# Attention block on one core: the last group and the last feed-forward tiles in an order written by hand, the residual in W_base's diagonal, weight preparation at another unit

## The chip, the cores and the metric

The kernel runs on one core of a Trainium2 chip. The metric is the time of one execution on the device in microseconds (us). Three plain executions took 703.10, 703.36 and 704.18 us, median 703.36. A further execution was taken by the hardware profiler; all durations of single instructions are from that one.

## What is computed

Two batches (b) of 512 tokens with 512 features go through causal attention with 32 query heads and 8 key/value heads of 128, then a residual and a layer norm, then a feed-forward part of one base matrix and eight low-rank experts that a sparsemax router weighs, then a residual and a layer norm again. Cut to what matters:

```python
x = hidden                                      # (2, 512, 512), f32
q, k, v = x @ Wq, x @ Wk, x @ Wv                # 32 / 8 / 8 heads of 128
p = softmax(causal(q @ k.T * 128**-0.5))
x = layernorm(x + (p @ v) @ Wo)
base = x @ W_base.T + b_base
w = sparsemax(x @ W_router.T + b_router)        # 8 experts
h = einsum('bsd,edr->bser', x, lora_A)          # rank 16
x = layernorm(x + base + einsum('bser,bse,ero->bso', h, w, lora_B))
```

## The kernel before

**Precision.** Products of the attention are split into a high and a low f16 half, and each is made of three matmuls (`mm3`, L223): high-high, high-low, low-high. After every product, `cut_psum` (L227, L228) splits the PSUM result again: ScalarE (ACT) writes the high half, VectorE (DVE) the low one. The feed-forward part uses f32r halves in the same way.

**Units.** A *group* (g, b) is one key/value head g with its four query heads on one batch, a *unit* (g, b, i) the 128 query rows of tile i in it, so there are 64 units. The groups run as (0,0), (0,1), (1,0) ... (5,1), and then (6,0), (7,0), (6,1), (7,1); in the last group i goes from 3 down to 0, so that the largest tile comes first. Three functions make a unit:
- `unit_a` (L309): for four heads, the scores `s` (3 matmuls each, into 4 PSUM buffers "S"), mask and maximum on VectorE (L325), exp on ACT (L330); after every second head the reciprocal of the sums (L336, L338), the cut into `phl`, and a DMA transpose into `pt` on SyncE's queue (SP).
- `unit_b` (L353): `pv` from `pt` and `vt`, then its cut `o`.
- `unit_c` (L373): `pw` from `o` and Wo's rows, and `acc += pw * factor` on VectorE (L384). `acc` starts as x, so the residual is in it.

In step s the loop (L668) issues `unit_a` of unit s, a part of the next group's projections (`proj`, k, q, v), `unit_b` of unit s-1 and `unit_c` of unit s-2. A scheduler of the language decides the order on each engine from there, except in the first group's start, which stands in a block with a written order (L536).

**Weights.** `prepare` (L152) loads a group's six projection matrices (JS) or four Wo rows (ROWS) in raw form, takes the largest absolute value of each (`amax`, L118, VectorE), squares these on ACT (L180), adds over partitions with a matmul with ones (`tot`, L123, PE), makes scales of them (L128 to L133) and has GpSimd (POOL) scale and split the weights (L112 to L115). `plan` and `at` (L629 to L659) tell at which unit each step of such a generator is issued. `sync_load` ties a load behind the third-last transpose. `behind(engine)` (L407) ties what is issued in it behind the last instruction of that engine so far.

**Feed-forward.** After a tile's last `unit_c`, `ffn` (L422) is stepped once per place in the loop: layer norm statistics (L413 to L415, the power on POOL, L417), normalise (L420), `px`: four transposes, three copies (L431 to L433), POOL adds the bias to `acc` (L434), `pb`: LoRA and router product (L437), the router's sparsemax in ten small VectorE instructions (L453 to L463), `phw` and `h` (L469 to L472), `pa`: the base product and the LoRA product in one PSUM tile, `acc += pa` on VectorE (L477), layer norm to `y`, store on SP (L480). Tiles 0 to 3 are of batch 0 and run beside batch 1's attention; tiles 4 to 7 follow the last group, in the order 7, 6, 5, 4. In the profile's names `lna` and `lnb` are the first and second layer norm.

Of the kernel before, what the change touches and what calls it, by code (L numbers as in the profile page):

```python
# [8 lines left out]
F32 = mybir.dt.float32  # L9
# [27 lines left out]
def kernel(  # L37
# [131 lines left out]
    def measure(g, js, raws, name, rows, n):  # L169
        mx = sb.tile([P, 8], F32, tag="mx", name=f"mx{name}", bufs=2)  # L170
        for k, (j, raw) in enumerate(zip(js, raws)):
            j = k + 1 if rows else j
            amax(mx[:, j : j + 1], raw)
            if k % 2:
                yield
        sc = sb.tile([P, 2, 8], F32, tag="sc", name=f"sc{name}", bufs=8)
        if rows:
            amax(mx[:, 0:1], mx[:, 1:5])
        sq = sb.tile([P, 8], F32, tag="sq", name=f"sq{name}", bufs=2)
        nc.scalar.activation(sq[:, :n], mx[:, :n], AF.Square)  # L180
        scales(sc, total(sq, n, name), n)
        SC[(g, rows)] = sc
        yield
# [122 lines left out]

    PT = {}

    def unit_a(g, b, i):  # L309
        n = P * (i + 1)  # L310
        k2, lm = KT[(g, b)], LM[(g, b)]
        phl = sb.tile([P, 2, 2, 2, n], F16, tag="PHL", name=f"phl{g}_{b}_{i}", bufs=2)
        pt = sb.tile([P, 2, 2, 2, i + 1, P], F16, tag="PT", name=f"pt{g}_{b}_{i}", bufs=2)
        es = []
        st = sb.tile([P, 4, HPG], F32, tag="ast", name=f"ast{g}_{b}_{i}", bufs=3)
        for h in range(HPG):
            q2 = QT[(g, b, h)]
            sc = ps.tile([P, S], F32, tag="S", name=f"s{g}_{b}_{i}_{h}", bufs=4)
            qs = slice(i * P, (i + 1) * P)
            mm3(sc[:, :n], [  # L320
                (q2[:, 0, qs], k2[:, 0, :n]),
                (q2[:, 0, qs], k2[:, 1, :n]),
                (q2[:, 1, qs], k2[:, 0, :n]),
            ])
            nc.vector.tensor_tensor_reduce(  # L325
                out=sc[:, :n], in0=sc[:, :n], in1=mask[:, S - n :], scale=lm[:, h : h + 1], scalar=BIG,
                op0=ALU.add, op1=ALU.min, accum_out=st[:, 0, h : h + 1],
            )

            nc.scalar.activation(  # L330
                sc[:, :n], sc[:, :n], AF.Exp, bias=st[:, 0, h : h + 1], scale=-1.0, accum_out=st[:, 1, h : h + 1]
            )
            es.append(sc)
            if h % 2 == 0:
                continue
            nc.vector.reciprocal(st[:, 2, h - 1 : h + 1], st[:, 1, h - 1 : h + 1])  # L336

            nc.vector.scalar_tensor_tensor(  # L338
                st[:, 3, h - 1 : h + 1], st[:, 2, h - 1 : h + 1], 32768.0, sc[:, :2], ALU.mult, ALU.max
            )  # L340
            pair = h // 2
            for j in range(2):
                k = 2 * pair + j
                cut_psum(phl[:, pair, 0, j, :], phl[:, pair, 1, j, :], es[k][:, :n], st[:, 3, k : k + 1])

            sync_transpose(
                pt[:, pair].rearrange("p a h t q -> p (a h t) q"), phl[:, pair].rearrange("p a h n -> p (a h n)")
            )
        PT[(g, b, i)] = pt

    OT = {}

    def unit_b(g, b, i):  # L353
# [4 lines left out]
        for kt in range(i + 1):  # L358
            vh, vl = vt[:, kt, :], vt[:, NT + kt, :]
            ph, pl = pt[:, :, 0, :, kt, :], pt[:, :, 1, :, kt, :]  # L360
            pairs += [(vh, ph), (vh, pl), (vl, ph)]
        mm3(pv, pairs)
        o2 = sb.tile([P, 2, HPG, P], F16, tag="O", name=f"o{g}_{b}_{i}", bufs=2)
        cut_psum(o2[:, 0], o2[:, 1], pv, 2.0**-15)
        OT[(g, b, i)] = o2

    def out_factor(g, b):
        lm = LM[(g, b)]
# [4 lines left out]
    def unit_c(g, b, i, first):  # L373
# [5 lines left out]
        for h in range(HPG):  # L379
            w2 = W[(g, 6 + h)]  # L380
            pairs += [(o2[:, 0, h, :], w2[:, 0, :]), (o2[:, 0, h, :], w2[:, 1, :]), (o2[:, 1, h, :], w2[:, 0, :])]
        mm3(pw, pairs)
        a = acc[b * NT + i]
        nc.vector.scalar_tensor_tensor(a, pw, LM[(g, b)][:, 7:8], a, ALU.mult, ALU.add)  # L384

    F = {}

    def ffn_setup():
        base = [sb.tile([P, KC, HID], F32R, tag=f"base{q}", name=f"base{q}") for q in range(2)]
        for c in range(KC):  # L390
            split(base[0][:, c, :], base[1][:, c, :], load_raw(w_base[:, c, :], f"base{c}"))
            yield
        lar = sb.tile([P, KC, NL], F32, tag="lar", name="lar")
        sync_load(lar, lar_in)
# [13 lines left out]

        return tc.issue_after(next(i for i in reversed(nc.cur_bb.bb.instructions) if i.engine == engine))

    def layernorm(dst, src, name, tail):
        st = sb.tile([P, 12], F32, tag="lnst", name=f"ln{name}", bufs=2)
        nc.vector.bn_stats(st[:, 0:6], src)  # L413
        nc.vector.bn_aggr(st[:, 6:8], st[:, 0:6])
        nc.vector.tensor_scalar(st[:, 9:10], st[:, 7:8], EPS, None, ALU.add)  # L415
        with tc.high_priority():
            nc.gpsimd.tensor_tensor(st[:, 8:9], st[:, 9:10], cmh, ALU.pow)  # L417
        yield
        with nullcontext() if tail else behind(mybir.EngineType.DVE):
            nc.vector.tensor_scalar(dst, src, st[:, 6:7], st[:, 8:9], ALU.subtract, ALU.mult)  # L420

    def ffn(t, tail):  # L422
        base, lar, lb, bias, kk = F["base"], F["lar"], F["lb"], F["bias"], F["k"]
        a = acc[t]
        yield from layernorm(a, a, f"a{t}", tail)
        px = ps.tile([P, KC, P], F32, tag="S" if tail else "wo", name=f"px{t}", bufs=4 if tail else 1)
        for c in range(KC):
            nc.tensor.transpose(px[:, c, :], a[:, c * P : (c + 1) * P], ident)
        xf = sb.tile([P, KC, P], F32, tag="xf", name=f"xf{t}")
        x2 = sb.tile([P, 2, KC, P], F32R, tag="x2", name=f"x2{t}")  # L430
        nc.scalar.copy(xf, px)  # L431
        nc.scalar.copy(x2[:, 0], px)
        nc.vector.tensor_tensor(x2[:, 1], px, f(x2[:, 0]), ALU.subtract)  # L433
        nc.gpsimd.tensor_tensor(a, a, bias[:, :HID], ALU.add)  # L434
        yield
        pb = ps.tile([P, NL], F32, tag="S" if tail else "pj", name=f"pb{t}", bufs=4 if tail else 2)
        mm3(pb, [(xf[:, c, :], lar[:, c, :]) for c in range(KC)])  # L437

        def base_part():
            pa = ps.tile([P, HID], F32, tag="pj", name=f"pa{t}", bufs=2)  # L440
            pairs = []
            for c in range(KC):
                xh, xl = x2[:, 0, c, :], x2[:, 1, c, :]
                pairs += [(xh, base[0][:, c, :]), (xh, base[1][:, c, :]), (xl, base[0][:, c, :])]
            mm3(pa, pairs, last=False)
            return pa

        if tail:
            pa = base_part()
        r = sb.tile([P, 6, NE], F32, tag="rt", name=f"rt{t}", bufs=2)  # L450
        s = sb.tile([P, 4], F32, tag="rs", name=f"rs{t}", bufs=2)
        z, zs, zc, sup, tmp, w = (r[:, j, :] for j in range(6))
        nc.vector.tensor_tensor(z, pb[:, NE * NR :], bias[:, HID:], ALU.add)  # L453
        nc.vector.max(zs, z)
        nc.vector.tensor_tensor_scan(zc, zs, zs, 0.0, ALU.add, ALU.bypass)
        nc.vector.tensor_tensor(tmp, zs, kk, ALU.mult)
# [7 lines left out]
            hw, pb[:, : NE * NR].rearrange("p (e r) -> p e r", e=NE),  # L464
            w.unsqueeze(2).broadcast_to([P, NE, NR]), ALU.mult,
        )
        yield
        ph = ps.tile([P, P], F32, tag="S" if tail else "wo", name=f"phw{t}", bufs=4 if tail else 1)
        nc.tensor.transpose(ph, hw.rearrange("p e r -> p (e r)"), ident)  # L469
        h2 = sb.tile([P, 2, P], F32R, tag="h2", name=f"h2{t}")  # L470
        nc.scalar.copy(h2[:, 0, :], ph)
        nc.vector.tensor_tensor(h2[:, 1, :], ph, f(h2[:, 0, :]), ALU.subtract)  # L472
        yield
        if not tail:
            pa = base_part()
        mm3(pa, [(h2[:, 0, :], lb[:, 0, :]), (h2[:, 0, :], lb[:, 1, :]), (h2[:, 1, :], lb[:, 0, :])], first=False)
        nc.vector.tensor_tensor(a, a, pa, ALU.add)  # L477
        y = sb.tile([P, HID], F32, tag="y", name=f"y{t}", bufs=2)
        yield from layernorm(y, a, f"b{t}", tail)
        nc.sync.dma_start(out_rows[t], y)  # L480
        yield

    live = []

# [138 lines left out]

    def step_live():

        step_ffn(s < len(units) - NT + LC)


    plan = {u: [] for u in range(-1, len(units) + 3)}  # L629
# [23 lines left out]
    for g in range(1, NG):  # L653
        u = NT * (starts[g] - 2) - (3 if g == NG - 2 else 0)
        if g > 1:
            at(prepare(g, JS), u - 1, u, u, u + 1, u + 2, u + 2, u + 3, u + 3, u + 3)
        u += NT
        if g > 1:
            at(prepare(g, ROWS), u - 1, u, u + 1, u + 2, u + 2, u + 3, u + 3)  # L659
# [1 line left out]
    def advance(last=False):  # L661
        while plan.get(s):
            next(plan[s].pop(0), None)
            if not last:
                break

    LB, LC = 1, 2
    for s in range(len(units) + LC):  # L668
        if s < len(units):
            g, b, i = units[s]  # L670
            k = s // NT
            nx = groups[k + 1] if k + 1 < len(groups) else None
            if s == NT:
                load_x(1)
            unit_a(g, b, i)
            step_live()
            if nx:
                for j in ((4, 0), (1,), (5,), (2, 3))[i]:
                    proj(*nx, j)
                    advance()  # L680
            step_live()
        if s >= LB and s - LB < len(units):
            unit_b(*units[s - LB])
            step_live()
            advance()
        if s >= LC:
            n = s - LC
            u = units[n]
            unit_c(*u, n % NT == 0)
            step_live()  # L690
            if u == (NG - 1, 1, NT - 1):
                while live:
                    step_ffn(True)
            if u[0] == NG - 1:
                live.append(ffn(u[1] * NT + u[2], u[1] == NB - 1))
        advance(True)
    while live:
        step_ffn()


_OUTS = [((2, 512, 512), "float32")]
# [51 lines left out]
```

## Time and profile before

| what | value |
|---|---|
| plain executions | 703.10, 703.36, 704.18 us, median 703.36 |
| the profiled execution | 707.78 us |
| its span, first to last instruction | 705.7 us, 10,943 instructions |
| chain that ended last, by engine | PE 78%, DVE 8%, DMA 5%, issue 3%, ACT 3%, POOL 2% |
| its costliest lines | pw 20%, pq 18%, pv 13%, s 11%, pk 5%, pvp 5%, pa 2% |
| granted TensorE clock, mean | 0.995 of full |
| DMA issues on SP | 128 transposes of p (3.8 us from issue to landing), loads of 256 KB (3.0 to 5.2 us), 8 stores (2.0 us) |

Engines in the profile: PE is TensorE's matmul, PEld its weight load, DVE VectorE, ACT ScalarE, POOL GpSimd, SP SyncE. A row of a timeline is: start, duration, engine, line, operation, output <- inputs, shapes, count of merged instructions, and in brackets how long the engine was idle before and what ended that. A row of the view of waits is: the waiting engine, its tile and line, what it waited for, then the sum in us, the count, and the longest.

### The profile page before, as it was taken

Reading aid. Unit: us, or ns where it says so; the run is one execution under the profiler, and the core shown is the slowest. Engines: PE = TensorE matmul, PEld = TensorE weight load, DVE = VectorE, ACT = ScalarE, POOL = GpSimd, SP = SyncE. Lnnn points to the kernel's source line nnn. Section 1 sums busy time; section 2 is a strip of 40 time slices with the busy share of each in tenths; the row PEclk is TensorE's granted clock in tenths of the full one; section 3 lists DMA queues with packets and bytes.
Section 4 is the critical chain, followed back from the end, with each engine's and each line's share of the span. In section 5 each row is a group of like instructions: output and inputs, shape, how many; then the busy total and the mean of one; then the engine's idle time right before and its main releaser. Section 6 shows DMA issues by size and latency. Waiting matters only on the chain.

```text
span 705.7 us, 10943 instructions
## 1 busy us (share of the span) xinstructions
PE 681.4 (97%) x3434; PEld 351.9 (50%) x3434; DVE 534.4 (76%) x1604; ACT 366.4 (52%) x1010; POOL 241.3 (34%) x331
## 2 busy tenths in 40 slices
PE   8999999999999999999999999899999999998895
PEld 4764545454544545454444545354544554554463
DVE  5797787867777786867777868767785786878775
ACT  5875745555464555545554556345464563445410
POOL 7665450725026240825034193134322010100131
PEclk9999999999999999999999999999999999999999
DMA  8659382637456373856368362916443251435301
GB/s 322 178 117 193 78 201 47 140 76 173 75 109 142 65 183 42 174 111 150 75 129 185 62 148 48 199 24 149 75 91 74 56 106 32 93 62 117 61 16 45
DMA packets 202026, 78.08 MB, mean 111 GB/s; under 512 B 186736, under 2 KB 186736, under 8 KB 201968
## 3 DMA queue, kind: packets, MB, share of 16 engines
q1 hardware_dynamic: 201680, 76.85, 49.7%
q10 hardware_dynamic: 288, 0.52, 0.3%
q8 instruction: 27, 0.44, 0.3%
q14 instruction: 31, 0.25, 0.1%
HBM read 29.12 MB, written 2.10 MB: 44 GB/s over the span
## 4 chain that ended last, share of the span: by engine, by line
PE 78%; DVE 8%; DMA 5%; issue 3%; ACT 3%; POOL 2%; SPq 0%; POOLq 0%; DVEq 0%; ACTq 0%
PE pw L223 20%; PE pq L223 18%; PE pv L223 13%; PE s L223 11%; PE pk L223 5%; PE pvp L223 5%; PE pa L223 2%; DVE phl L228 2%; PE park L223 2%; DMA raw<-in_wv_dram 1%; DMA pt<-phl 1%; ACT s L330 1%; PE pb L223 1%; DVE acc L384 1%; DVE s L325 1%
## 5 line engine op out<-in xcount | busy, mean ns | idle before, releaser
L330 ACT ACTIVATE s<-s,ast 128x128 f32<-128x128 f32 (+3 forms) x256 | 127.7, 499 | 170.0 <-DVE ast L325 168.2
L223 PE MATMUL pw<-w,o 128*128 128x512 f16 x768 | 176.9, 379 | 1.3 <-DVE acc L384 1.3
L223 PE MATMUL pq<-xT,w 128*128 128x512 f16 x672 | 153.9, 382 | 2.6 <-DVE q L228 2.6
L223 PEld LDWEIGHTS <-w 128*128 128x128 f16 x1008 | 98.3, 98 | 115.2 <-issue 5.9
L227 ACT ACTIVATE phl<-s,ast 128x128 f16<-128x128 f32 (+3 forms) x256 | 116.8, 539 | 37.7 <-issue 20.0
L228 DVE SCALAR_TENSOR_TENSOR phl<-s,ast,phl 128x128 f16<-128x128 f32 (+3 forms) x256 | 125.0, 545 | 3.9 <-ACT phl L227 2.2
L325 DVE CUSTOM_DVE_ANT_0 s<-s,mask,lm 128x128 f32<-128x128 f32 (+3 forms) x256 | 126.7, 555 | 1.3 <-PE s L223 1.2
L223 PE MATMUL s<-k,q 128*128 128x128 f16 (+3 forms) x768 | 117.9, 299 | 4.7 <-DVE phl L228 3.9
L223 PEld LDWEIGHTS <-o 128*128 128x128 f16 x768 | 74.8, 98 | 91.2 <-issue 2.4
L223 PE MATMUL pv<-pt,vt 128*128 128x512 f16 x480 | 114.5, 379 | 2.7 <-DMA pt<-phl 2.7
L223 PEld LDWEIGHTS <-q 128*128 128x128 f16 x768 | 68.4, 98 | 53.1 <-issue 7.2
L255 POOL TENSOR_SCALAR lm<-sc,xs 128x1 f32<-128x1 f32 x15 | 4.0, 264 | 235.8 <-DVE sc L132 144.3
L115 POOL TENSOR_TENSOR w<-raw,w 128x512 f16<-128x512 f32 x68 | 77.2, 1154 | 0.3
L223 PEld LDWEIGHTS <-vt 128*128 128x128 f16 x480 | 46.8, 100 | 56.6 <-DMA pt<-phl 3.4
L384 DVE SCALAR_TENSOR_TENSOR acc<-pw,lm,acc 128x512 f32<-128x512 f32 x64 | 47.9, 749 | 31.8 <-PE pw L223 31.7
L228 DVE SCALAR_TENSOR_TENSOR o<-pv,o 128x512 f16<-128x512 f32 x64 | 43.9, 686 | 31.1 <-ACT o L227 31.0
L112 POOL TENSOR_SCALAR raw<-raw,sc 128x512 f32<-128x512 f32 x68 | 46.3, 691 | 59.7 <-DVE sc L133 59.6
L118 DVE TENSOR_REDUCE mx<-raw 128x1 f32<-128x512 f32 x66 | 44.3, 681 | 29.4 <-DMA raw<-in_wo_dram 13.3
L227 ACT ACTIVATE o<-pv 128x512 f16<-128x512 f32 x64 | 39.5, 617 | 32.3 <-PE pv L223 32.3
L330 ACT ACTIVATION_READ_ACCUMULATOR s<-s,ast 128x1 f32 x256 | 51.5, 201 | 0.0
L228 DVE SCALAR_TENSOR_TENSOR q<-pq,q 128x512 f16<-128x512 f32 x56 | 38.4, 687 | 14.6 <-ACT q L227 14.5
L227 ACT ACTIVATE q<-pq 128x512 f16<-128x512 f32 x56 | 34.0, 611 | 18.7 <-PE pq L223 18.7
(125 smaller groups left out, 613.0 us busy)
## 6 DMA issues: line engine op xcount, KB each, us to landing
raw<-in_wo_dram SPq DMA_DIRECT2D x32, 256.0 KB, 3.6
raw<-in_wq_dram SPq DMA_DIRECT2D x28, 256.0 KB, 4.6
raw_x<-in_xt_dram SPq DMA_DIRECT2D x8, 256.0 KB, 4.7
acc<-in_x_dram SPq DMA_DIRECT2D x8, 256.0 KB, 4.6
pt<-phl SPq DMA_TRANSPOSE x128, 3.8
out_dram<-y SPq DMA_DIRECT2D x8, 256.0 KB, 2.0
raw<-in_wk_dram SPq DMA_DIRECT2D x7, 256.0 KB, 3.0
raw<-in_wv_dram SPq DMA_DIRECT2D x7, 256.0 KB, 4.6
```

The costliest lines, as they stand in the source:

```text
L112: nc.gpsimd.tensor_scalar(view, view, by, 1.0, ALU.mult, ALU.mult)
L115: return first.ins, nc.gpsimd.tensor_tensor(lo, view, hi, ALU.subtract).ins
L118: nc.vector.tensor_reduce(dst, view, AX.X, ALU.max, apply_absolute_value=True)
L223: nc.tensor.matmul(dst, a, b, start=first and j == 0, stop=last and j == n - 1)
L227: nc.scalar.activation(hi, psrc, AF.Copy, scale=by)
L228: return nc.vector.scalar_tensor_tensor(lo, psrc, by, hi, ALU.mult, ALU.subtract).ins
L255: engine.tensor_scalar(lm[:, 4:5], sc[:, 0, 4:5], XS[b][0], 1.0, ALU.mult, ALU.mult)
L325: nc.vector.tensor_tensor_reduce(out=sc[:, :n], in0=sc[:, :n], in1=mask[:, S - n :], scale=lm[:, h : h + 1], scalar=BIG, op0=ALU.add, op1= ...
L330: nc.scalar.activation(sc[:, :n], sc[:, :n], AF.Exp, bias=st[:, 0, h : h + 1], scale=-1.0, accum_out=st[:, 1, h : h + 1])
L384: nc.vector.scalar_tensor_tensor(a, pw, LM[(g, b)][:, 7:8], a, ALU.mult, ALU.add)
```

## The change

1. **The tail.** The loop ends four units earlier (`len(units) - NT`). The last group's units, the last parts of the group before it, the feed-forward of tile 3 and of tiles 4 to 7 are cut into pieces and issued in the order of a list of tokens, `TAIL`, in a block in which each engine keeps the written order. `unit_a`, `unit_b` and `unit_c` become generators for that; the ordinary loop runs them through with `done`.
2. **The residual** goes into the base matrix: the identity is added to W_base's diagonal before it is split, so `pa` holds the residual too. For tiles 0 to 2 one VectorE addition of `pa` and the bias replaces L434 and L477. For tiles 3 to 7 the bias enters PSUM as two matmuls of a one-partition row (`bias_row`), and statistics and normalise read `pa` in PSUM. The base product's order becomes xh with base0, xh with base1, xl with base0, four matmuls each, and the low half of x is made on VectorE (`low`, tile 7) or on POOL (`low_pool`, tiles 3, 4, 5 and 6).
3. **Weights.** The JS generator's first step is put at unit u-2, where it was at u-1 (for group 6 it stays), and JS's maxima of groups 2 to 7 are issued behind VectorE's last instruction.

```diff
@@ measure
-            amax(mx[:, j : j + 1], raw)
+            with behind(mybir.EngineType.DVE) if g > 1 and not rows else nullcontext():
+                amax(mx[:, j : j + 1], raw)
...
@@ ffn_setup
-            split(base[0][:, c, :], base[1][:, c, :], load_raw(w_base[:, c, :], f"base{c}"))
+            raw = load_raw(w_base[:, c, :], f"base{c}")
+            diag = raw[:, c * P : (c + 1) * P]
+            nc.gpsimd.tensor_tensor(diag, diag, ident, ALU.add)
+            split(base[0][:, c, :], base[1][:, c, :], raw)
...
+    def low_pool(t):
+        px, xf, xh, xl = X[t]
+        nc.gpsimd.tensor_tensor(xl, xf, f(xh), ALU.subtract)
...
+    def base_part(t, last):
...
+        pairs = list(F["row"]) if last else []
+        for x2, r in ((xh, 0), (xh, 1), (xl, 0)):
+            pairs += [(x2[:, c, :], base[r][:, c, :]) for c in range(KC)]
+        mm3(PA[t], pairs, last=False)
...
+    def store(t, src, st):
+        y = sb.tile([P, HID], F32, tag="y", name=f"y{t}", bufs=2)
+        normalize(y, src, st)
+        nc.sync.dma_start(out_rows[t], y)
...
-            at(prepare(g, JS), u - 1, u, u, u + 1, u + 2, u + 2, u + 3, u + 3, u + 3)
+            at(prepare(g, JS), u - (1 if g == NG - 2 else 2), u, u, u + 1, u + 2, u + 2, u + 3, u + 3, u + 3)
...
+    def bias_row():
...
+        split(rows[0][0:1, :], rows[1][0:1, :], bias)
+        nc.gpsimd.tensor_scalar(rows[2][0:1, :P], ones[0:1, :], 1.0, 1.0, ALU.mult, ALU.mult)
+        F["row"] = [(rows[2][0:1, :P], rows[q][0:1, :]) for q in (0, 1)]
...
+    TAIL = """
+    n3 a7 N3 p7 q7 B7 C6 O7 x3 D6 a6 r3 C7 L3 s3 p6 q6 b7 o7 a5 D7 m3 p5 q5 h3 c7 a4 b6 d7 p4 o6
+    n7 e3 N7 q4 c6 x7 d6 b5 n6 f3 r7 l7 o5 m7 N6 s7 c5 d5 h7 x6 b4 e7 n5 o4 f7 N5 r6 L6 c4 F7 d4
+    F3 x5 s6 n4 m6 h6 L5 r5 N4 s5 e6 f6 m5 h5 F6 x4 e5 L4 r4 s4 f5 m4 h4 F5 e4 f4 F4
+    """
...
-    for s in range(len(units) + LC):
+    for s in range(len(units) - NT):
...
-    while live:
-        step_ffn()
+        if s == len(units) - 2 * NT:
+            bias_row()
+    while live:
+        step_ffn(True)
+    with tc.manual_schedule(engines={ET.PE, ET.DVE, ET.Activation, ET.Pool, ET.SP}):
+        tail()
```

The tokens, with the tile's number behind: a scores with mask, maximum and exp; p and q the cut and transpose of the first and second pair of heads; b and o `pv` and its cut; c and d `pw` and its addition to `acc`; B, O, C, D the same for the group before the last; n and N first statistics and normalise; x the transposes and copies; l and L the low half of x on VectorE or POOL; r `pb`; s the router; m the base product; h `phw` and `h`; e the LoRA product; f and F second statistics, and normalise with store.

## Prediction

> **What bounds the kernel now.** I read the page first: busy times, then the row of slices.
>
> ```profile
> PE 681.4 (97%) x3434; PEld 351.9 (50%) x3434; DVE 534.4 (76%) x1604; ACT 366.4 (52%) x1010; POOL 241.3 (34%) x331
> PE   8999999999999999999999999899999999998895
> ```
>
> TensorE (PE) is the bound: 24 us of 705.7 are idle. So the question for every edit is which PE wait it ends. The last three slices are the weak ones. I then took PE's busy time by stretch (columns: length, PE, PEld, DVE, ACT, POOL busy with counts, clock, DMA):
>
> ```profile
> 400.00:450.00 50.00, 50.00 (x254) 24.20 (x253) 38.71 (x113) 27.93 (x78) 24.35 (x32) 1.00 0.56 123
> 450.00:500.00 50.00, 47.42 (x241) 22.82 (x240) 38.17 (x108) 23.86 (x66) 23.81 (x32) 0.97 0.52 105
> ...
> 635.00:650.00 15.00, 12.66 (x63) 7.21 (x61) 13.14 (x45) 10.34 (x26) 1.27 (x1) 1.00 0.52 106
> 650.00:665.00 15.00, 13.18 (x76) 6.79 (x75) 11.57 (x42) 6.82 (x26) 0.98 (x2) 1.00 0.49 88
> 665.00:680.00 15.00, 13.11 (x64) 7.58 (x64) 10.94 (x33) 3.91 (x9) 3.96 (x5) 1.00 0.13 35
> 680.00:690.00 10.00, 9.62 (x55) 7.54 (x54) 7.35 (x35) 1.83 (x4) 3.61 (x4) 1.00 0.01 4
> 690.00:698.00 8.00, 7.22 (x35) 5.22 (x33) 5.21 (x22) 1.12 (x3) 0.55 (x1) 1.00 0.09 33
> ```
>
> Most stretches of the body are full; 450 to 500 is not, and its clock fell. From 635 to 698 PE is busy 55.8 of 63 us, so 7.2 us are idle. Each wait also hides the drain of the matmul before it (a 512-column f16 matmul lasts 0.38 us but the next starts 0.216 us after it). Counted from start to start in the timeline, the waits from 635 on sum to 10.1 us: 1.4 + 0.5 before the scores of tile 6, 1.4 around px3 and pb3, 0.3 before pw of tile 6, 1.8 for the transposes of tile 5, 0.8 before pb7, 1.3 before pw of tile 4, 1.9 around the last four LoRA steps, and 0.6 in three small ones.
>
> The waits in the body come from the view of who waited for whom, and then from the timeline around the largest:
>
> ```profile
> DVE mx L118 <- DMA raw<-in_wk_dram: 12.0, 6, 3.0
> DVE mx L118 <- DMA raw<-in_wq_dram: 4.0, 6, 1.3
> ...
> PE pq L223 <- DVE q L228: 2.6, 1, 2.6
> ```
>
> ```profile
> 450.44 0.69 DVE L118 TENSOR_REDUCE mx<-raw 128x1 f32<-128x512 f32 x1 [0.86 <-DMA raw<-in_wq_dram]
> 451.04 1.40 DVE L228 SCALAR_TENSOR_TENSOR phl<-s,ast,phl 128x512 f16<-128x512 f32 x2
> 452.36 0.15 DVE L338 SCALAR_TENSOR_TENSOR ast<-ast,s 128x2 f32<-128x2 f32 x1
> 452.42 0.69 DVE L228 SCALAR_TENSOR_TENSOR q<-pq,q 128x512 f16<-128x512 f32 x1
> ...
> 453.16 4.44 PE L223 MATMUL pq<-xT,w 128*128 128x512 f16 x12 [2.58 <-DVE q L228]
> ```
>
> The maxima of the next weights stand in VectorE's queue in the middle of a softmax and wait there for a load; the softmax and the cut of q queue behind; PE's next projection waits for the cut's buffer. PE loses 2.7 us start to start, and the twelve matmuls after the gap take 4.44 us where such a dozen takes 2.75: 1.7 us at half clock. The same pattern costs PE 2.2 us at 101.6 to 102.9 and 1.2 us at 337 to 338 (first scores of a group, third matmul waiting for q's low half).
>
> **The change, part by part.** I compared the order of instructions per engine before and after.
>
> *Maxima and "loads one unit sooner".* In SP's order no load moves, and its waits are the same; so no load starts sooner. What moves is VectorE's 36 maxima of groups 2 to 7 (0.68 us each, same count): they now stand behind the next unit's cuts, about 6 to 10 us later (the first of group 2 was at 94.5, its load had landed by then; the last of the six loads is issued at 94.13 and such loads land 3 to 4.7 us after issue). So the 16 us that VectorE waited for wk and wq end. Gain on PE: 2.2 + 1.2 + 2.7 + 1.7 = 7.8 us. What is late next: the Wo maxima keep their place and still wait (13.3 us in ten waits); behind them the third score matmul found q's low half done only 0.58 us early at 141.9, 0.88 at 220, 0.40 at 377, 1.04 at 460. A PE that is 2 us earlier can run into these. Loads follow PE's own progress, so most of the slack moves along. Bounds of what is given back: 0 (all moves along) and 7.8 (PE loses at each what it won). I take 2.0, some 0.4 at each of five places. Body: -5.8 us.
>
> *The Pool queue.* Added: four 128x128 additions of the identity (nearest row 0.52 us each) and three one-partition operations, against eight 1.27 us additions of the bias that go. POOL is 34% busy, and w's first tile is ready 9.2 us before its projection (132.8 against 142.0), so this costs nothing; without that cover it would be 2 us once.
>
> *The tail's written order.* PE does every product as before plus ten one-row matmuls (bias, two for each of five tiles). No row has one partition; bounds are 0 and 0.235 us (spacing of pa's), and I take 0.23: +2.3 us. The 10.1 us of waits are rearranged. Following the new order engine by engine with the rows' durations, these stay: 0.5 before tile 6's scores (cut of tile 7's second pair), 0.3 for tile 7's transposes, 1.7 before tile 5's third score (VectorE's cuts of tile 6 free the buffer; the same release cost 1.4 at 638.5), 1.0 before pw of tile 6 (0.60 ACT and 0.69 DVE behind pv, with three matmuls of 0.23 between), 0.1 before px7, 0.4 before the last pb, 0.7 before the last LoRA product (ACT h, 0.6 now): 4.7 us. Bounds: 0, and 10.1 as now. So -10.1 + 4.7.
>
> *The end behind the last matmul.* Now:
>
> ```profile
> 697.55 1.12 PE L223 MATMUL pa<-lorab,h 128*128 128x512 f32 x3 [0.35 <-ACT h L471]
> 698.71 0.69 DVE L477 TENSOR_TENSOR acc<-acc,pa 128x512 f32<-128x512 f32 x1
> ...
> 701.66 0.55 POOL L417 TENSOR_TENSOR lnb<-lnb,cmh 128x1 f32<-128x1 f32 x1 [0.79 <-DVE lnb L415]
> 702.25 0.55 DVE L420 TENSOR_SCALAR y<-acc,lnb 128x512 f32<-128x512 f32 x1 [0.73 <-POOL lnb L417]
> ```
>
> 698.67 to 702.80 is 4.1 us: two tiles' ends share VectorE. Afterwards only tile 4 is left there: statistics from PSUM 0.69, aggregate 0.17, add 0.15, power 0.55, normalise, and about 0.25 of handing over. The normalise lasts 0.54 now from SBUF; from PSUM no row shows it. Bounds 0.54 and 0.75 (acc<-pw, which reads PSUM); nearest are the 512-element cuts from PSUM, 0.69. Sum 2.5 us, so -1.6. Five L477 additions (0.68) go from VectorE; beyond the last one that is in the waits above. The store itself (2.0 us) stays.
>
> [...] The trace: while a 0.54 us normalise ran, POOL's power took 0.84 instead of 0.55 (633.4) and its bias addition 1.48 instead of 1.27 (678.1). [...] The change puts four 1.27 us subtractions on POOL. By the rows that costs at most 4 x 0.3 = 1.2, off PE's path for three; I take 0. [...]
>
> The clock: here it halved after a gap of about 2.9 us. [...]
>
> **Sum.** Tail -10.1 + 4.7 + 2.3 - 1.6 = -4.7. Body -5.8. Together -10.5 on the profiled execution's own 707.78 us (span 705.7, 2.1 around it): 697.3. The plain runs have a median of 703.36, 4.4 less than that execution, and no row says where. Whether the half clock is in them is open, so I count half of its 1.7: -9.7, which makes **693.7**. A difference under 0.2% (1.4 us) can't be told from none here.
>
> **Rivals.**
> 1. *Tail alone.* The body's waits return at the Wo maxima. For: slack there is only 0.4 to 1.0. Against: slack stayed alike over four groups. 703.4 - 4.7 = 698.7. Chance 0.15.
> 2. *Body alone.* A written order holds each engine to it; one late head (PE behind VectorE's route chain, some 2 us of small operations) brings the 10.1 back. -5.0 + 2.3 - 1.6 = -4.3: 699.1. Chance 0.10.
> 3. *All of it*, nothing given back and the clock included: -4.7 - 7.8 = -12.5, 690.9; a little more if the waits in the tail end as well (to 688). Chance 0.12.
> 4. *Slower.* PE holds the sum of squares (tot, L123) at a fixed place in its order, which does not move. Its input is ready 20 to 24 us early now (104.9 against 125.0); with the maxima up to 10 us later, and the last pair behind another unit's cut, I leave 3 to 4 us. If the maxima are over 4 us later than I follow them, PE stands at six places; with 2 us each, 12 - 4.7 = +7.3: 710.7. Chance 0.05.
> 5. *No difference*: the gains are in the profile alone. 703.4. Chance 0.04.
> Forecast (691 to 697): chance 0.54. The range 689.0 to 699.0 takes in rival 1, most of 3 and half of 2: 0.54 + 0.15 + 0.10 + 0.05 = 0.84. Faster by over 0.2%: 0.54 + 0.15 + 0.10 + 0.12 = 0.91; same 0.04; slower 0.05.
>
> **What would show it.** Right: no wait of VectorE's maxima for wk and wq; no PE gap over 1.5 us after 60 and a clock of 1.00 at 450 to 500; the last store issued 2.5 us behind the last matmul; one-row matmuls spaced 0.23. Wrong: PE waiting at tot, third score matmuls waiting behind Wo maxima by over 1 us, POOL subtractions near 1.8 us with PE behind them, or tail waits of 8 us and more.

## The result, and the profile after

The changed kernel took **696.97 us** (median of 4 runs, 696.06 to 698.76) beside 703.77 us for the kernel before (4 runs, 703.1 to 706.09): ratio 0.9894, 95% interval 0.9872 to 0.9917. The forecast was 693.7 us in a range from 689.0 to 699.0. The profiled execution took 697.11 us, span 694.9.

From the page of the kernel after, the busy line and PE's 40 slices:

```profile
PE 681.7 (98%) x3444; PEld 353.1 (51%) x3444; DVE 534.5 (77%) x1595; ACT 367.1 (53%) x1010; POOL 239.9 (35%) x334
PE   8999999999999999999999999999999999999996
```

PE's busy time is the same in sum (681.4 before), so only idle time went: 13 us are left of 24. The weak slices at the end are full but for the last, in which PE's work ends.

The same stretches as before, those of the tail taken 11 us sooner, as the kernel is by then (columns: length, busy us and instructions of PE, PEld, DVE, ACT, POOL, then clock, DMA share, GB/s):

```profile
400.00:450.00 50.00, 50.00 (x254) 24.18 (x253) 40.51 (x114) 27.76 (x76) 22.82 (x31) 1.00 0.62 138
450.00:500.00 50.00, 50.00 (x262) 24.44 (x260) 38.38 (x112) 25.32 (x76) 23.61 (x31) 1.00 0.51 100
624.00:639.00 15.00, 14.79 (x76) 7.50 (x74) 13.17 (x42) 9.17 (x23) 2.33 (x3) 1.00 0.42 87
639.00:654.00 15.00, 13.64 (x74) 8.13 (x75) 11.31 (x46) 8.31 (x28) 0.00 (x0) 1.00 0.54 89
654.00:669.00 15.00, 14.63 (x73) 8.74 (x73) 11.46 (x38) 4.66 (x11) 1.70 (x4) 1.00 0.09 18
669.00:679.00 10.00, 10.00 (x52) 6.71 (x51) 8.59 (x26) 1.36 (x4) 4.25 (x5) 1.00 0.14 54
679.00:689.00 10.00, 9.51 (x45) 6.98 (x44) 7.10 (x35) 1.60 (x4) 2.36 (x3) 1.00 0.07 27
```

450 to 500 is full and at full clock. From 624 to 689 PE is idle for 2.4 of 65 us where it was 7.2 of 63.

Of the maxima's waits in the view of who waited for whom, the lines for `raw` from wk and wq are gone, and that for Wo stayed (13.3 us before):

```profile
DVE mx L118 <- DMA raw<-in_wo_dram: 14.6, 13, 2.4
```

The place at 453 us, in after's timeline (start, duration, engine, line, operation):

```profile
444.94 2.73 DVE L229 SCALAR_TENSOR_TENSOR phl<-s,ast,phl 128x512 f16<-128x512 f32 x4 [0.23 <-ACT phl L228]
447.07 1.46 PE L224 MATMUL pw<-w,o 128*128 128x512 f16 x6
447.58 0.68 DVE L229 SCALAR_TENSOR_TENSOR q<-pq,q 128x512 f16<-128x512 f32 x1
448.37 2.75 PE L224 MATMUL pq<-xT,w 128*128 128x512 f16 x12
```

No maximum stands between the softmax's cuts; q is cut at 447.58 and the twelve matmuls start with no idle time and take 2.75 us (4.44 before). One thing the prediction did not tell: the order written by the scheduler also has three more matmuls of `pw` ahead of these twelve (six where there were three), 0.65 us of work that now lies in the former gap. weights_only below has the same six.

And the end:

```profile
688.44 0.96 PE L224 MATMUL pa<-lorab,h 128*128 128x512 f32 x3 [0.35 <-ACT h L504]
689.44 0.70 DVE L429 BATCH_NORM_STATS2 lnf<-pa 128x6 f32<-128x512 f32 x1
690.62 0.55 POOL L433 TENSOR_TENSOR lnf<-lnf,cmh 128x1 f32<-128x1 f32 x1 [2.47 <-DVE lnf L431]
691.20 0.81 DVE L437 TENSOR_SCALAR y<-pa,lnf 128x512 f32<-128x512 f32 x1 [0.66 <-POOL lnf L433]
```

From the last matmul's end (689.40) to that of the normalise (692.01) it is 2.6 us, 4.1 before.

**A cleaner measure.** The timed runs of one kernel spread over several us, so the traces are compared by three stretches, cut at two products that stand at a fixed place in PE's order: the start of `tot` (L123) at 83 to 85 us and the last one, at 514 to 521 us. *Body* is between the two, *tail* from the second to the end of the span. All in us, from the timelines; the last column is the timed median of the runs.

| kernel | start | body | tail | span | timed |
|---|---|---|---|---|---|
| before, first profile | 83.8 | 437.3 | 184.6 | 705.7 | 703.77 |
| before again | 84.1 | 433.5 | 184.4 | 702.0 | 704.0, one run; 705.05 / 704.73 / 703.83 beside the three groups below |
| early_only | 83.8 | 434.1 | 184.6 | 702.5 | 703.98 |
| tail_only | 83.9 | 435.8 | 180.95 | 700.7 | 700.60 |
| weights_only | 83.6 | 430.2 | 184.1 | 697.8 | 699.98 |
| after | 83.8 | 430.2 | 180.96 | 694.9 | 696.97 |
| after_again | 85.4 | 430.4 | 181.00 | 696.8 | 699.18 |
| after_third | 83.3 | 430.4 | 180.91 | 694.5 | 698.04 |
| m3_first | 84.2 | 430.5 | 181.7 | 696.3 | 697.60 |
| low_dve | 83.7 | 430.0 | 184.3 | 698.1 | 697.18 |
| no_bias | 83.6 | 430.5 | 179.3 | 693.3 | 695.36 |
| split_only | 83.9 | 430.5 | 180.4 | 694.8 | 697.01 |
| bias_dve | 83.8 | 430.3 | 182.7 | 696.8 | 699.63 |
| split_mixed | 83.9 | 430.0 | 182.3 | 696.2 | 698.76 |

With the maxima moved, the body is 430.0 to 430.5 in all ten profiles; three profiles of after agree on the tail within 0.1. So a difference of 0.3 us in a stretch means something, where one of 1.5 us between timed medians may not. The change is -3.65 in the tail, and -3.3 to -7.1 in the body, by which execution of the kernel before it is held against.

### The profile page after: what moved, and what is told of

Same layout as the page of the kernel before. It is cut to its first block, busy times and chain, and to the rows that moved or that the text cites. A ratio compares the mean times of both kernels' runs of the same rounds, so it can differ in the third digit from the quotient of the medians.

```text
span 694.9 us, 10948 instructions
## 1 busy us (share of the span) xinstructions
PE 681.7 (98%) x3444; PEld 353.1 (51%) x3444; DVE 534.5 (77%) x1595; ACT 367.1 (53%) x1010; POOL 239.9 (35%) x334
## 4 chain that ended last, share of the span: by engine, by line
PE 82%; DVE 8%; DMA 3%; ACT 3%; issue 2%; POOL 2%; POOLq 0%; DVEq 0%; ACTq 0%; SPq 0%
PE pw L224 20%; PE pq L224 19%; PE pv L224 13%; PE s L224 11%; PE pk L224 6%; PE pvp L224 5%; PE pa L224 4%; DVE phl L229 3%; PE park L224 2%; DVE s L342 1%; DMA raw<-in_wo_dram 1%; ACT s L347 1%; PE pb L224 1%; DMA pt<-phl 1%; ACT phl L228 1%
## 5 line engine op out<-in xcount | busy, mean ns | idle before, releaser
L224 PE MATMUL pq<-xT,w 128*128 128x512 f16 x672 | 152.2, 379 | 0.0
L118 DVE TENSOR_REDUCE mx<-raw 128x1 f32<-128x512 f32 x66 | 42.8, 678 | 14.7 <-DMA raw<-in_wo_dram 14.6
```

What stands on the lines that cost most here:

```text
L118: nc.vector.tensor_reduce(dst, view, AX.X, ALU.max, apply_absolute_value=True)
L224: nc.tensor.matmul(dst, a, b, start=first and j == 0, stop=last and j == n - 1)
```

## The experiments

The kernels ran in three groups of four, each group on a chip of its own beside the kernel before. A theory and a rival are what was expected before the run; a ratio is the kernel's time over that of the kernel before on the same chip, with its 95% interval.

### The body: which edit, and how much of it in a timed run

**before_again**: the kernel before, unchanged.

> The kernel before, unchanged, profiled a second time, for its profiled execution is 3.6 to 4.7 us above its timed runs. Theory A (the halved clock at 453 to 457 us belongs to the profiled execution and not to the timed ones): this second profile shows no halved clock inside the body, and its span is 702 to 704 us; then the gap at 453 us is worth under 2.7 us in the timed runs and the change gains less there than in the profile. Theory B (the gap and the halved clock are in every execution): span 705 to 707 us with a granted clock below 1 near 455 us, and the distance between profile and timed runs has another cause.

704.0 us, span 702.0. Its place at 453 us, and below it that of tail_only, which has the same order there:

```profile
451.35 2.75 PE L223 MATMUL pq<-xT,w 128*128 128x512 f16 x12 [1.54 <-DVE q L228]
```

```profile
451.78 4.44 PE L223 MATMUL pq<-xT,w 128*128 128x512 f16 x12 [2.39 <-DVE q L228]
```

The same instruction waits 1.54 us in one execution, 2.39 in another and 2.58 in the first profile; after 1.54 the dozen takes 2.75 us, after the two others 4.44 at half clock (a mean of 0.56 from 453 to 456 us in the first profile and 0.59 in tail_only; here 1.00 from 451 to 457). Theory A holds for this execution, but B is not dead: both happen. 49 timed runs of the kernel before, 45 of them beside these groups, spread from 702.0 to 709.7 us. The granted clock of these 45 goes with their time: at a mean of 0.991 or 0.992 they took 705.6 to 709.7 us, at 0.997 or 0.998 702.0 to 705.7.

**weights_only**: both edits on the weights, and nothing else.

```
 before:  amax(mx[:, j : j + 1], raw)
+         with behind(DVE) if g > 1 and not rows else nullcontext():
+             amax(mx[:, j : j + 1], raw)
-         at(prepare(g, JS), u - 1, u, u, ...)
+         at(prepare(g, JS), u - (1 if g == NG - 2 else 2), u, u, ...)
```

> Before with the two edits on the weights alone (the maxima behind the subtractions, and one unit sooner); the order of the tail, and the base product's place, stay. Theory (the body's three gaps at 101, 337 and 453 us were waits of VectorE's maxima for loads, and go): span 5.5 to 7.5 us under the kernel before's profile, the tail as before at 82 to 83 us from the first score of the last group; timed 2.5 to 6 us under the kernel before (697.5 to 701). Rival (the gaps are in the profile only, or come back elsewhere): timed within 1.5 us of the kernel before, and the tail alone then carries the gain.

699.98 us; ratio to before 0.9926 (0.9898 to 0.9953). Body 430.2, tail 184.1: the whole gain is in the body. Its six runs lie between 699.75 and 700.22, where before has 702.74 to 709.68 beside them. That the wait for the loads was what made the runs differ is not shown: after lacks it too, and its runs spread over 1.7 to 3.1 us.

**early_only**: the second of the two edits alone.

> Before with the first step of each preparation one unit sooner, and nothing else. Theory (that edit changes the order of no engine, and no load starts sooner; the weights' gain is all from the maxima standing behind the subtractions): no difference from the kernel before, ratio 0.998 to 1.002, gaps at 101, 337 and 453 us as before. Rival (the sooner step moves the loads): the waits of VectorE's maxima for loads fall below 10 us in sum and the time by 2 us and more.

703.98 us beside 704.73: ratio 0.9981 (0.9962 to 1.0), and a body of 434.1. Its view of who waited for whom:

```profile
DVE mx L118 <- DMA raw<-in_wk_dram: 11.5, 6, 2.6
DVE mx L118 <- DMA raw<-in_wq_dram: 3.5, 5, 1.8
```

The waits are there (15.0 us in sum). "One unit sooner" alone does nothing, so the gain needs the maxima's place (that edit alone was not run). Instruction by instruction, the order is that of the kernel before on all five engines.

**tail_only**: after, with both edits on the weights taken back.

> After with both edits on the weights taken back: the written order of the tail and the base product alone. Theory: the tail takes 3.6 to 4.7 us less than before's 82.6 us, timed 699 to 700 us, and the body keeps its gaps at 101, 337 and 453 us. Rival (the body's gain is nothing in timed runs): timed 696.5 to 697.5, as fast as after. Rival (the tail's gain is nothing in timed runs): 702 to 704.

700.60 us; ratio 0.9939 (0.9916 to 0.9961). The tail is after's (180.95), the body is before's with the gap of 2.39 us and its halved clock (0.84 from 450 to 453 us, 0.59 from 453 to 456). By stretches the two halves of the change add up to 0.1 us. Timed they don't: 5.07 and 4.45 make 9.5, and after is 5.6 to 6.8 under before. A timed median takes in the start too, and the kernel before moves in its body; which of them makes the difference was not traced.

**after_again, after_third**: after, unchanged, in the two later groups.

> After, unchanged, in the same call as the kernels below, so that they are compared on one chip. 696.0 to 698.5 us. Theory (the body's gap at 453 us was the varying part of the kernel before, 1.7 us in one profile of it and 2.7 plus a halved clock in the other): the timed runs of after lie within 1 us of each other but for single ones, where the kernel before spreads over 7 us. Rival (the spread comes from the chip whatever the kernel): after spreads over several us too.

> After, unchanged, in the same call as the three below. From the squares of group 3 on, the trace runs as in the two profiles of after: 430.2 to 430.4 us from the sum of squares at 83.8 to the last one at 514.0, and 180.9 to 181.0 us from there to the end; what differs is the first 84 us. Theory (one loading of the same kernel differs from another in the start, by up to 2 us, and nowhere else): 696 to 700 us timed, whatever the start shows is the difference. Rival (the difference is in the body or the tail): one of these two stretches is off by over 0.5 us.

699.18 us (0.9912, 0.9895 to 0.993), above what was expected, and 698.04 us (0.9913, 0.9894 to 0.9933). The rival of after_again has some truth: after spreads too, over 3 us in after_third (696.53 to 699.59). In the three profiles body and tail repeat within 0.2 us; it is the start that moves. In after_again a wait of 2.07 us at 33.5 us is followed by half clock, 0.91 from 30 to 35 and 0.75 from 35 to 40, and `tot` comes 1.6 us later than in after. This had nothing to do with the change: no edit touches the order of those first 60 us.

### The tail: what the ten one-row matmuls cost

**no_bias**: after, with an empty list in place of the two one-row products in `base_part`.

> After without the two one-row products of the last five tiles, ten matmuls in all (so the base bias is left out of those tiles' output). Theory (each takes 0.23 us of TensorE's own time, on the path): timed 1.9 to 2.6 us under after, 694.4 to 695.1, and the span likewise. Rival (they lie in waits that are there without them): within 0.7 us of after.

695.36 us; ratio to before 0.9861 (0.9833 to 0.9889); tail 179.26, so 1.70 less than after's. The last base product, in after and then in no_bias:

```profile
683.17 1.19 PE L224 MATMUL pb<-lar,xf 128*128 128x136 f32 x8
684.29 0.73 PE L224 MATMUL pa<-brow,brow 1*128 1x512 f32 x2
684.95 3.02 PE L224 MATMUL pa<-base,x 128*128 128x512 f32 x12
687.81 0.27 PE L502 MATMUL phw<-ident,hw 128*128 128x128 f32 x1
```

```profile
682.06 1.19 PE L224 MATMUL pb<-lar,xf 128*128 128x136 f32 x8
683.00 3.01 PE L224 MATMUL pa<-base,x 128*128 128x512 f32 x12
685.85 0.27 PE L502 MATMUL phw<-ident,hw 128*128 128x128 f32 x1
```

From the start of `pb` to that of `phw`, with no wait between, it is 4.64 us with the pair of rows and 3.79 without: **0.85 us a pair, 0.43 a matmul**. The theory had 0.23. Over the five places, start to start, it is 4.1 us of PE. Leaving them out gives only 1.7, since 2.2 come back as waits: 0.5 and 0.7 where `phw` waits for VectorE's `hw` (no such line in after), 0.4 at `pw` of tile 6, 0.3 in tile 7's base product, and 0.3 behind the last matmul, where the normalise of tile 5's `y` on VectorE stands ahead of the last statistics. Both theories are half right: the cost is larger than the theory's, and a good half of it lies in waits, as the rival says.

**bias_dve**: no rows; VectorE adds the bias, and statistics and normalise read SBUF.

```
+ nc.vector.tensor_tensor(acc[t], PA[t], F["bias"][:, :HID], ALU.add)
- stats["f", t] = statistics(PA[t], ...);  store(t, PA[t], stats["f", t])
+ stats["f", t] = statistics(acc[t], ...); store(t, acc[t], stats["f", t])
```

> After with the base bias added by VectorE (one 512-element addition for each of the last five tiles, 0.69 us, PSUM to SBUF, with the statistics and the normalise reading SBUF) in place of the ten one-row matmuls. Theory (the ten rows cost PE 1.65 us net, as leaving them out showed; behind the last matmul the addition adds 0.69, and statistics and normalise from SBUF give 0.1 and 0.25 back): tail 1.3 us shorter than after's 180.95, at 179.5 to 179.9. Rival (five more additions make VectorE late for PE's next buffers, as it was before the change): tail 180.9 or longer.

699.63 us (0.9939, 0.992 to 0.9958), tail 182.74: 1.8 **longer** than after's. The theory fell. From its waits:

```profile
PE phw L502 <- DVE hw L493: 2.1, 2, 1.5
PE pa L224 <- DVE h L505: 0.9, 2, 0.5
PE pa L224 <- DVE x L455: 0.8, 1, 0.8
```

and from its timeline:

```profile
660.44 0.68 DVE L772 TENSOR_TENSOR acc<-pa,ffnbias 128x512 f32<-128x512 f32 x1
...
672.23 1.28 POOL L459 TENSOR_TENSOR x<-xf,x 128x512 fp32r<-128x512 f32 x1
672.29 1.51 DVE L437 TENSOR_SCALAR y<-acc,lnf 128x512 f32<-128x512 f32 x1 [0.44 <-POOL lnf L433]
```

VectorE is late for two reasons. One is the five additions of 0.68 us. The other: a normalise of y of 0.55 us took 1.51, having started just behind a subtraction on POOL, and at 684.52 another did the same. Start to start against no_bias, PE loses 0.7 us in tile 7's base product, 0.6 before the second-last LoRA product and 0.6 behind the last matmul, each time with an addition in front on VectorE (660.44, 681.97, 690.89) and no subtraction beside it. It loses 1.2 at tile 6's `phw` and 0.6 before the last LoRA product, where an addition and a stretched normalise of y both stand in front, and wins 0.3 back at the last `pb`. How those two divide was not tried. After has a stretched normalise too, of `acc` (bias_dve has it as well, at 678.60), and beside another subtraction one that is not stretched:

```profile
671.59 1.27 POOL L459 TENSOR_TENSOR x<-xf,x 128x512 fp32r<-128x512 f32 x1
671.65 0.81 DVE L437 TENSOR_SCALAR y<-pa,lnf 128x512 f32<-128x512 f32 x1 [0.44 <-POOL lnf L433]
...
677.46 1.27 POOL L459 TENSOR_TENSOR x<-xf,x 128x512 fp32r<-128x512 f32 x1
677.53 1.49 DVE L437 TENSOR_SCALAR acc<-acc,lnn 128x512 f32<-128x512 f32 x1 [0.52 <-POOL lnn L433]
```

Both began 0.06 to 0.07 us behind POOL. The one that reads PSUM takes its 0.81 us; the one that reads SBUF ends 0.3 us after POOL does. So the rows cost less than the additions do: with the bias on PE, VectorE is spared five additions, and the normalise of y reads PSUM, 0.26 us dearer alone but not stretched here.

**low_dve**: `L3 L6 L5 L4` written as `l3 l6 l5 l4`, so VectorE makes those low halves.

> After with the four subtractions that make the low half of tiles 3 to 6 on VectorE (0.55 us each in the rows of such a cut) where after has them on GpSimd (1.27 us each). Theory (they lie beside other work, and GpSimd's cost the path nothing): within 0.6 us of after. Rival (GpSimd's longer subtraction is what the last tiles' products wait for, at 0.7 us a tile on the path): 1 to 2.5 us under after.

697.18 us beside after_again's 699.18, but with runs in two heaps: 696.74 to 697.31 four times, 699.31 and 700.03. The mean clock of these two is 0.993 and 0.994, that of the four 0.995 to 0.998. The profiled one is of the second heap. Its stretches from 642 us:

```profile
642.00:645.00 3.00, 1.73 (x12) 1.05 (x11) 2.26 (x7) 1.54 (x3) 0.00 (x0) 0.99 0.43 82
645.00:648.00 3.00, 3.00 (x9) 1.78 (x7) 2.79 (x12) 2.02 (x9) 0.00 (x0) 0.50 0.98 181
648.00:651.00 3.00, 3.00 (x9) 2.32 (x8) 1.95 (x6) 1.58 (x4) 0.00 (x0) 0.50 0.16 33
```

With the low half of tile 3 on VectorE, tile 5's first scores wait 0.53 us (0.11 in after), just ahead of the 1.3 us wait for the third; the clock then halves until 651.8. Start to start, low_dve is 3.7 us behind after at 651.71, most of it by the half clock, and 3.4 at the end, all that the tail is longer than after's. As in the expectation's first theory, GpSimd's subtractions cost the path next to nothing: the normalise that POOL stretches in after takes 0.55 in low_dve (at 681.05), but in after the `hw` behind it is ready 0.5 us before PE takes it. The 0.3 us that low_dve wins back is a wait before the last `pb` in after; why low_dve lacks it is open.

**m3_first**: `o7 a5 D7 m3 p5` written as `o7 m3 a5 D7 p5`.

> After with one place of the written order changed: tile 3's base product stands ahead of tile 5's scores and not behind them and tile 7's cut. Theory (tile 5's third score waits 1.3 us at 644 us for a score buffer which tile 6's cuts free; 1.6 us of base product ahead of it fill that wait): 0.8 to 1.5 us under after. Rival (the wait is for VectorE's cuts, which are late wherever PE stands, and what follows tile 5's scores comes 1.6 us later): within 0.5 us of after, the wait turning up at tile 7's or tile 6's next product.

697.60 us beside 699.18, but its tail is 0.7 *longer* than after's; of the profiles, after_again's start is 1.2 us longer, so the timed difference can't be put down to the edit. The wait at 644 us is gone and stands one product further on:

```profile
649.10 2.10 PE L224 MATMUL pw<-w,o 128*128 128x512 f16 x9 [1.37 <-DVE acc L396]
```

The rival holds, and the tail is a little worse than it said: the wait is for VectorE's chain, and the place in PE's order only chooses which product waits.

**split_only**: the four low matmuls of the last base product behind the transpose of `hw`.

```
-    F7 ... f5 m4 h4 F5 e4 f4 F4
+    F7 ... f5 m4 h4 w4 F5 e4 f4 F4      (w4: xl x base[0], cut out of m4)
```

> After with the last base product cut in two: its four low matmuls stand behind the transpose of the last LoRA product's input and not ahead of it. Theory (PE waits 0.5 us before the last LoRA product for ScalarE's and VectorE's cuts, with nothing left to do; 0.94 us of matmuls fill it, and the transpose's input has been ready for 1.3 us): the tail from the last sum of squares is 0.4 to 0.6 us shorter than after's 180.95. Rival (the cuts come no sooner, being behind the statistics of tile 5 on VectorE): no change in the tail.

697.01 us beside 698.04 (ratios to before 0.9907, 0.9888 to 0.9926, and 0.9913, 0.9894 to 0.9933). The tail is 180.36, 0.6 shorter, as expected:

```profile
687.28 0.27 PE L506 MATMUL phw<-ident,hw 128*128 128x128 f32 x1
687.31 1.17 PE L224 MATMUL pa<-base,x 128*128 128x512 f32 x4
688.32 0.85 PE L224 MATMUL pa<-lorab,h 128*128 128x512 f32 x3
```

The last LoRA product no longer waits. By the trace it is the best version of this study that leaves nothing out; the timed runs alone can't tell it from after.

**split_mixed**: split_only, with the rows for the last tile alone and VectorE's addition for the four others.

> Both at once, the better version by the theories: the one-row matmuls stay for the last tile alone (two of ten), VectorE adds the bias for the four others, and the last base product is cut in two. Theory: tail 1.5 to 2.1 us shorter than after's 180.95 (8 of 10 rows at 1.65 us net, plus 0.5), 178.9 to 179.5. Rival (VectorE becomes late): within 0.5 us of split_only's tail.

698.76 us (0.9933, 0.9913 to 0.9952), tail 182.29: 1.9 longer than split_only's. The theory fell, and VectorE is late as the rival says, by more than its 0.5 us: the trace has four additions and the same two stretched normalises of y (at 672.14 and 684.37) as bias_dve.

## Why the prediction was right, and where it was off

The direction, the mechanism and the range were right; the forecast was 3.3 us too low, and two of its terms, the passage to the plain runs and the one-row matmuls, were off the same way. By its own steps:

- *PE's idle time is what counts.* Right: busy time unchanged, 11 us of idle time gone from the span.
- *No load starts sooner; the maxima's place does it.* Right (early_only 0.9981, with the same waits).
- *Body -5.8 on the profiled execution.* It was -7.15: the 2.0 us to be given back at the Wo maxima are 0.6 (0.29 at 140 and 0.26 at 296.5 us). **The step that is off most is the passage to the plain runs, "I count half of its 1.7".** The second profile of before has no half clock there, and the gaps themselves are smaller: the three places cost 1.5, 0.9 and 1.7 us, not 2.2, 1.2 and 2.7. So 4.0 - 0.6 = 3.4 were to be had, and 3.3 to 3.9 came by the bodies of before_again and early_only, against the 4.95 counted: about 1.4 of the 3.3 us. That is by profiles. The plain runs' mean clock (0.991 to 0.998, median 0.995) tells that many had some half clock, not where, and the 5.07 of weights_only, 3.3 to 7.2 by its interval, fits 3.4 as well as 4.95.
- *Ten one-row matmuls at 0.23.* The term was mis-sized: 4.1 us and not 2.3, so 0.41 each over the five places. The bound, the spacing of full matmuls, was no bound: 0.34 and 0.32 us pass from start to start of the two rows and the first full matmul behind them (a spacing of 0.23 was to show the forecast right), and the first row starts 0.21 us after the last `pb`, where a full matmul starts after 0.03 without rows.
- *Waits that stay, 4.7.* About 4.0: 0.5 before tile 6's scores (0.5 forecast), 0.4 for tile 7's transposes (0.3), 1.5 at tile 5's third score (1.7), 0.7 at `pw` of tile 6 (1.0), 0.1 before px7 (0.1), 0.3 before the last `pb` (0.4), 0.5 before the last LoRA product (0.7). Following a written order by the rows' durations works to a few tenths.
- *End, 2.5 us.* 2.6; the normalise from PSUM took 0.81, over its upper bound of 0.75.
- *Tail -4.7.* -3.65. The rows cost 1.8 more, the waits that stay 0.7 less, the end 0.1 more: together -3.5.
- *POOL's subtractions cost nothing.* True of the time to 0.3 us, with the size of one meeting wrong: where a subtraction met a normalise from SBUF, the normalise lost 0.94 us, not the 0.3 of the rows used. In after that was hidden; in bias_dve it is part of what made PE wait for `hw`. In both, the normalise ended 0.3 us after POOL's subtraction did. From PSUM it took 0.81 beside POOL, as alone. Why the two differ no run shows.
- *Rival 4, PE at tot.* Its margin was right and just enough: group 2's squares end at 118.6 and PE takes them at 122.8, 4.2 us (3 to 4 forecast); no wait there in any profile.
- *What is left.* 703.36 less 3.3 to 3.9 and 3.65 makes 695.8 to 696.4; measured 696.97. The rest is within the 2.1 us by which the start varies in profiles. What sets the start of an execution was not tried.

Open: whether the three `pw` matmuls in front of the dozen at 448 us or the maxima behind the cuts ended that gap was not separated. An estimate from after's rows: without them PE would be there at 447.72 and q's cut ends at 448.26, so they cover some 0.6 us of the gap at most, and the maxima's place the rest. Nor was bias_dve tried with the low halves on VectorE, which would keep its normalises from meeting POOL.

## What to carry to other kernels

A profile is one execution: where an engine waits for a load, take the wait from several executions before pricing it (1.54, 2.39 and 2.58 us before one instruction here), and compare changes by stretches between fixed instructions, which repeat to 0.2 us in three profiles of after where its timed medians spread over 2. Price an instruction that no row shows with wider bounds than its nearest relative: a matmul with one row cost 0.41 to 0.43 us, nearly twice the 0.23 of a full one of `pa`. Moving work onto the bound engine can still pay (the rows: a tail of 181.0 us, 182.7 with the additions) if the second engine would make it wait for longer.

## What the runs showed of the hardware

- The clock halved after single idle times of TensorE of 2.07 (start of after_again), 2.39 and 2.58 us (at 452 and 453 us, tail_only and before), and in low_dve after waits of 0.53, 0.20, 1.26 and 0.20 us (start to start) within 3 us, with only a few matmuls between. It also halved between 5 and 10 us in tail_only, no_bias and bias_dve (a mean of 0.83, 0.82 and 0.74 there), which did not make their start longer (83.9, 83.6 and 83.8 us, 83.8 in after). It did not halve after 1.54 and 1.68 (at 451 us, before_again and early_only), 1.52 (bias_dve, 677 us) and 1.89 us (33 us, before_again).
- In the trace of the kernel before, the half clock ahead of the last matmul lasted 3.413 us, from 453.36 to 456.77. Counted from where the clock first became full, at 6.21 us, it began after 447.15 us, 131.0 times its length; a second one, behind the last matmul, began after 696.32 us, 204.0 times it, and that of after, counted likewise, after 686.08 us, 201.0 times. In the other profiles the windows' means give about 3.4 us for the half clock in after_again and in the body of tail_only, 3.4 to 3.5 us for those between 5 and 15 us, and 6.9 us for low_dve's. Whether these began at such multiples too, and whether the place of a wait among them counts, is not shown; nor is it settled how much idle time halves the clock.
- A normalise of 128x512 in f32 takes 0.55 us from SBUF and 0.81 from PSUM; beside a POOL subtraction of 1.27 us that started first, 1.49 to 1.51 from SBUF and 0.81 from PSUM.
- In three profiles of the same kernel, after, the first 84 us took 83.3 to 85.4 us and the rest repeated within 0.2. The kernel before moved by 3.8 us between two profiles, in its body (437.3 and 433.5).
